# The relu of q written to the scores' PSUM banks in the last segments of a recurrent attention

## The chip, the cores and the metric

The kernel runs on one core of one Trainium2 chip. The core has five engines with a queue of instructions each: TensorE (PE in the profile, with its weight loads as PEld), VectorE (DVE), ScalarE (ACT), GpSimd (POOL) and SyncE (SP, which issues most transfers). Work passes between them through SBUF and, for the results of matmuls, through PSUM, which has eight banks of 512 fp32 columns in each of 128 partitions. The metric is device time in microseconds (us), smaller is better, as the median of several runs.

## What is computed

Two layers, each an attention and a mixture of experts, multiplied and added to x: `x = x + attention(norm(x)) * silu(experts(norm(x)))`. The change lies in the attention of the first layer. It has 16 heads of 64 columns; a sequence of 512 tokens is cut into 8 segments of 64, and a memory M with its sum Z is carried from one segment to the next. For each segment, in the reference:

```python
scores = jnp.einsum('bhid,bhjd->bhij', q, k) * scale      # masked above the diagonal
att_dot = jnp.einsum('bhij,bhjv->bhiv', jax.nn.softmax(scores, axis=-1), v)
sq = jax.nn.elu(q) + 1.0
att_mem = sq @ M / (sq @ jnp.swapaxes(Z, -2, -1))
sk = jax.nn.elu(k) + 1.0
M_new = M + jnp.einsum('bhld,bhlv->bhdv', sk, v)
Z_new = Z + sk.sum(axis=-2, keepdims=True)
att = gate * att_mem + (1.0 - gate) * att_dot
out = att.reshape(B, LSEG, H * DV) @ Wo
```

There are 4 sequences, so 32 segments, numbered 0 to 31 through all of them.

## The kernel before

The function `attn0` (line 599) goes through the 32 segments in one loop, `for n in range(nseg)` (line 854). Every instruction is issued through small helpers (`mm1`, `act1`, `vec1`), which keep the order in which the program is written for each engine; nothing is reordered. The profile therefore shows line 356 for all matmuls and line 359 for all ScalarE operations, and one goes by the names of tiles. The loop is a pipeline by hand: in iteration n the scores and the q side of segment n+1 are begun, the memory is read for n, the k side is prepared for n+1 and n+2, and the outputs of n-2 are transposed.

One iteration, in the order of the code, with the names that the profile uses:

- `elu_exp(n + 1, 0)` (line 699): ScalarE makes exp(q) in the tile `elu` and relu(q) in the tile `up`, 128 x 512 each, both in SBUF. Two buffers serve all `up` tiles, of q and of k in turn.
- `scores(n + 1)` (line 673): 16 small matmuls write `sc`; VectorE caps the result into the tile `E` (line 686).
- `memory(n)` (line 746): matmuls `mm` of elu(q) with the memory `mz`; VectorE takes the reciprocals (`rm`, line 743) and the quotients into `t` (line 744); GpSimd multiplies by the gate (line 763).
- `elu(n + 1, 0)` (line 706): VectorE forms min(exp(q), 1) + relu(q), reading `elu` and `up` (line 709). The sum is elu(q) + 1.
- `turned(n - 2, n + 1)` (line 712): transposes `tn`, evicted by ScalarE into `attT` (four small operations) and `sk`.
- `update(n)` (line 765): matmuls `mu`, and VectorE adds them to the memory `mz` (line 778).
- `attend(n)` (line 780): matmuls `dot` of the exponentiated scores with v; VectorE divides (`rd`, `t`) and keeps the sums (line 800); GpSimd multiplies and adds (lines 801 and 802).
- `elu_exp(n + 2, 1)`, then `scores_exp(n + 1)`, then `elu(n + 2, 1)`: ScalarE makes exp and relu of k for the segment after next and the exp of `E`; VectorE finishes elu(k).
- In every fourth iteration `output` (line 816) multiplies four segments by Wo: 32 matmuls `po`. In the last iterations that is n = 26 and n = 30.

So ScalarE's queue holds, in each iteration: exp and relu of q for n+1, four `attT`, `sk`, exp and relu of k for n+2, exp of `E`. Segments 7, 15, 23 and 31 are the last of their sequence and need no k side.

Matmul results go to PSUM tiles of two banks, [128, 2, 512], from the function `wide` (line 367). Four such tiles fill PSUM, and each new one takes the place that was given up longest ago:

```python
    def wide(self, name):
        bufs = 4 if self.four else 3
        return self.banks.tile([P, 2, S], F32, name=name, tag="w", bufs=bufs)
```

The scores need columns 0 to 255 of each of their two banks; columns 256 to 511 are not used. An instruction that writes to a tile waits until the tile's place is free, and an instruction that depends on another engine's waits for that engine's semaphore count.

Of the kernel before, what the change touches and what calls it, by code (L numbers as in the profile page):

```python
# [12 lines left out]
F32 = mybir.dt.float32  # L13
# [3 lines left out]
AF = mybir.ActivationFunctionType  # L17
ALU = mybir.AluOpType
# [3 lines left out]
P = 128  # L22
# [80 lines left out]
def bc(ap, axis, n):  # L103

    shape = list(ap.shape)
    return ap.unsqueeze(axis).to_broadcast(shape[:axis] + [n] + shape[axis:])


class Kernel:
# [257 lines left out]
# [4 lines that stand above are left out]
# [228 lines left out]
    def attn0(self, xnT, g0, stack, between):  # L599
# [4 lines left out]
        nc, tc = self.nc, self.tc  # L604
# [4 lines left out]
        pool = stack.enter_context(tc.tile_pool(name="a0", bufs=2))  # L609
# [9 lines left out]
        for k in range(4):  # L619
            t = pool.tile([P, 4, 2, DK + 1], F32, name=f"vone{k}", bufs=1)  # L620
# [3 lines left out]
        wide = self.wide  # L624
# [44 lines left out]
        def blocks(n, w):  # L669
            s = n % 4  # L670
            return qkv[n // 4][w][:, s * 8 : s * 8 + 8, :]

        def scores(n):

            q, k = blocks(n, 0), blocks(n, 1)
            ps = wide(f"sc{n}")
            for hp in range(4):
                for p in range(2):
                    for a in range(2):
                        self.mm1(  # L680
                            ps[halves[a], p, hp * 64 : hp * 64 + 64],
                            lhsT=k[halves[p], 2 * hp + a, :], rhs=q[halves[p], 2 * hp + a, :],
                            start=True, stop=True,
                        )
            e = pool.tile([P, 2, 4, LSEG], F32, name=f"E{n}", tag="E")
            self.vec1(nc.vector.tensor_tensor(  # L686
                e, ps[:, :, 0:256].rearrange("p x (hp c) -> p x hp c", hp=4),
                bc(bc(self.cap, 1, 4), 1, 2), ALU.min,
            ))
            seg[n]["e"] = e  # L690

        def scores_exp(n):
            e = seg[n]["e"]
            self.act1(e, e, AF.Exp, scale=1.0 / math.sqrt(DK))

        def last(n):
            return n % 8 == 7

        def elu_exp(n, w):
            t = pool.tile([P, 8, 64], F32, name=f"elu{w}{n}", tag=f"elu{w}")  # L700
            up = pool.tile([P, 8, 64], F32, name=f"up{w}{n}", tag="up")
            self.act1(t, blocks(n, w), AF.Exp)
            self.act1(up, blocks(n, w), AF.Relu)
            seg[n][w] = t, up

        def elu(n, w):

            t, up = seg[n][w]
            self.vec1(nc.vector.scalar_tensor_tensor(t, t, 1.0, up, ALU.min, ALU.add))  # L709
            seg[n][w] = t  # L710

        def turned(att=None, own=None):

            ps = wide(f"tn{att}_{own}").rearrange("p x (w hp c) -> p x w hp c", w=2, hp=4)
            each = [(0, hp, x) for hp in range(4) for x in range(2) if att is not None]
            each += [(1, hp, x) for hp in range(4) for x in range(2) if own is not None]
            for w, hp, x in each:
                if w:
                    src = seg[own][1][halves[x], 2 * hp : 2 * hp + 2, :].rearrange("d a j -> d (a j)")
                else:  # L720
                    src = seg[att]["att"][halves[x], hp].rearrange("i p v -> i (p v)")
                self.pin(nc.tensor.transpose(ps[:, x, w, hp], src, self.ident[halves[x], halves[x]]))  # L722
            if att is not None:
                attended(att, ps[:, :, 0])
            if own is not None:
                t = seg[own]["sk"] = pool.tile([P, 4, 2, DK], F32, name=f"sk{own}", tag="sk")
                self.act1(t, ps[:, :, 1].rearrange("p x hp d -> p hp x d"), AF.Copy)

        def values(n):

            for p in range(2):
                src = vd[n // 4][p].rearrange("(s hp r) d -> s r hp d", s=4, hp=4)
                nc.sync.dma_start(out=vone[n % 4][:, :, p, 0:DK], in_=src[n % 4])
# [12 lines left out]
        def memory(n):  # L746


            mz, sq = self.mz[(n % 8 + 1) % 2 + 1 if n % 8 else 0], seg[n][0]
            ps = wide(f"mm{n}")  # L750
            for hp in range(4):
                for p in range(2):
                    for a in range(2):
                        at = (2 * a + hp // 2) * (DK + 1)
                        self.mm1(
                            ps[halves[(a + hp) % 2], p, at : at + DK + 1],
                            lhsT=sq[halves[p], 2 * hp + a, :], rhs=mz[halves[p], hp, a, :],
                            start=True, stop=True,
                        )
            t = seg[n]["t1"] = pool.tile([P, 4, 2, DK], F32, name=f"t1{n}", tag="t1")  # L760
            r = pool.tile([P, 2, 4], F32, name=f"rm{n}", tag="rm")
            divided(ps, t.rearrange("p hp y d -> p y hp d"), r, heads(ps)[:, :, :, DK])
            nc.gpsimd.tensor_mul(t, t, self.gate)  # L763

        def update(n):

            old = self.mz[(n % 8 + 1) % 2 + 1 if n % 8 else 0]
            new = self.mz[n % 2 + 1]
            sk, v = seg[n]["sk"], vone[n % 4]
            ps = wide(f"mu{n}").rearrange("p a (hp c) -> p a hp c", hp=4)[:, :, :, 0 : DK + 1]  # L770
            for hp in range(4):
                for a in range(2):
                    for p in range(2):
                        self.mm1(
                            ps[halves[p], a, hp], lhsT=sk[halves[a], hp, p], rhs=v[halves[a], hp, p],
                            start=True, stop=True,
                        )
            self.vec1(nc.vector.tensor_tensor(new, old, ps.rearrange("d a hp v -> d hp a v"), ALU.add))
# [37 lines left out]
        def output(h):  # L816
            ps = wide(f"po{h}")
            for c in range(16):
                for p in range(2):
                    self.mm1(  # L820
                        ps[:, p, 0:D], lhsT=attT[h][halves[p], c].rearrange("v s x -> v (s x)"),
                        rhs=self.wo[halves[p], c, :],
                        start=(c == 0), stop=(c == 15),
                    )
            two = slice(h * 2, h * 2 + 2)
            gate = g0[h // 2][:, h % 2 * 2 : h % 2 * 2 + 2, :]
            sg = pool.tile([P, 2, D], F32, name=f"sg{h}", tag="sg")
            self.vec1(nc.vector.tensor_tensor(sg, ps[:, :, 0:D], gate, ALU.mult))
            nc.gpsimd.tensor_add(self.x[:, two, :], self.x[:, two, :], sg)
# [24 lines left out]
        for n in range(nseg):  # L854
            if n % 4 == 3:
                todo = project((n + 1) // 4 + 1)
            elif n == 0:
                todo = ahead
            each = 2 if n == 0 else 4 if n < 3 or n % 4 != 2 else 0
            nxt = n + 1 < nseg  # L860
            more = nxt and not last(n + 1)
            if n + 2 < nseg:
                values(n + 2)
            if nxt:
                elu_exp(n + 1, 0)
                scores(n + 1)
            memory(n)
            if nxt:
                elu(n + 1, 0)
            if n > 1 or more:  # L870
                turned(n - 2 if n > 1 else None, n + 1 if more else None)
            if not last(n):
                update(n)
            for f, *args in between.get(n - 0.5, []):
                f(*args)
            attend(n)
            ahead = n + 2 < nseg and not last(n + 2)
            if ahead:
                elu_exp(n + 2, 1)
            chunks, todo = todo[:each], todo[each:]  # L880
            for chunk in chunks[:1]:
                chunk()
            if nxt:
                scores_exp(n + 1)
            if ahead:
                elu(n + 2, 1)
            for chunk in chunks[1:]:
                chunk()
            for f, *args in between.get(n - 0.25, []):
                f(*args)  # L890
            if n % 4 == 2 and n > 4:
                output(n // 4 - 1)
            if not nxt:
                turned(n - 1)
            for f, *args in between.get(n, []):
                f(*args)
# [1677 lines left out]
```

## Time and profile before

| | us |
|---|---|
| median of 3 runs | 689.84 |
| lowest and highest run | 688.49 and 690.34 |
| time of the profiled execution | 691.6 |
| span in its trace | 689.9 |
| TensorE busy | 656.5 (95%) |
| VectorE busy | 501.9 (73%) |
| ScalarE busy | 487.2 (71%) |
| GpSimd busy | 349.1 (51%) |
| the 60 elu operations, line 709 | 47.5, 0.791 each |
| the 60 relu operations, `up` | 38.4, 0.640 each |

The first attention runs from about 80 to 313 us of the span; the experts of the second layer follow. Busy times are averages over stages with different limits, so the prediction reads the stretch around the last segments by itself. A line of a timeline gives the start in us, the duration in us, the engine, the line, the operation, the tiles (written <- read), the shape and the count; in square brackets stands the idle time just before it and what ended it. An fp32 matmul appears as two records, so 16 matmuls of `sc` are shown as x32, and the weight loads are left out. Matmuls are pipelined: the duration of a merged group reaches to the end of its last result, and the next group can start before. A releaser is inferred from semaphores: where it had long been done, another one is meant.

### The profile page before, as it was taken

To read this page: it belongs to the slowest core of one execution; us is meant where nothing else is said; L and a number is where in the kernel's file an instruction comes from. 1 tells how busy PE (TensorE), PEld (TensorE's weight loads), DVE (VectorE), ACT (ScalarE), POOL (GpSimd) and SP (SyncE) were. 2 spreads that over 40 slices of the span, in tenths; PEclk is the share of its full clock that TensorE was granted. 3 is DMA by queue.
4 is the path that set the end of the run, shared out by engine and by line. 5 is a ranking of instruction groups with operands and counts; after the bars stand their busy time and mean duration, and the time that the engine had idled before them with its cause. 6 is when DMAs were issued, how large, how long until landed. Compare 5 with 4: busy or idle time off the path is not lost.

```text
span 689.9 us, 23790 instructions
## 1 busy us (share of the span) xinstructions
PE 656.5 (95%) x10123; PEld 411.0 (60%) x10123; DVE 501.9 (73%) x1084; ACT 487.2 (71%) x806; POOL 349.1 (51%) x383
## 2 busy tenths in 40 slices
PE   8999999999999898899999999999999999999995
PEld 4666667988978768777778863333335243422424
DVE  6866476686677958865378225979898999678884
ACT  4433478797787787643554369988997999899850
POOL 7590046767767575873753243312584753321170
PEclk9999999999999999999999999999999999999998
DMA  6850153233233131100034359777849694956300
GB/s 169 155 149 0 68 150 96 49 110 95 51 105 99 35 95 34 34 2 1 4 122 159 96 164 251 204 192 162 236 153 212 154 243 133 223 137 164 77 17 20
DMA packets 85489, 79.72 MB, mean 116 GB/s; under 512 B 42640, under 2 KB 74160, under 8 KB 82304
## 3 DMA queue, kind: packets, MB, share of 16 engines
q1 hardware_dynamic: 82544, 75.39, 41.5%
q0 software_dynamic: 2256, 2.47, 1.9%
q8 instruction: 82, 1.34, 0.8%
q10 hardware_dynamic: 576, 0.26, 0.2%
q14 instruction: 31, 0.25, 0.1%
HBM read 51.62 MB, written 26.21 MB: 113 GB/s over the span
## 4 chain that ended last, share of the span: by engine, by line
PE 74%; DVE 14%; ACT 8%; DMA 2%; issue 1%; POOL 0%; SPq 0%; DVEq 0%; ACTq 0%; POOLq 0%
PE acc L356 9%; PE eo L356 8%; PE pp L356 7%; ACT e L359 7%; PE po L356 6%; PE ph L356 5%; PE pv L356 4%; PE b L356 3%; PE s L356 3%; PE pl L356 3%; PE dot L356 2%; PE pg L356 2%; PE pu L356 2%; PE sc L356 2%; DVE elu L709 2%; PE mu L356 2%
## 5 line engine op out<-in xcount | busy, mean ns | idle before, releaser
L359 ACT ACTIVATE e<-s 128x1024 f32<-128x1024 f32 x124 | 122.2, 1059 | 14.5 <-PE s L356 14.1
L356 PE MATMUL acc<-e,strip 128*32 128x512 f32 x1000 | 123.7, 598 | 0.9 <-DVE e L1969 0.9
L359 ACT ACTIVATE e<-e 128x1024 f32<-128x1024 f32 x104 | 107.4, 1095 | 0.0
L763 POOL TENSOR_TENSOR t<-t,gate 128x512 f32<-128x512 f32 x32 | 52.3, 1634 | 52.8 <-DVE t L744 52.8
L356 PEld LDWEIGHTS acc<-e,strip 128*32 128x32 f32 x1000 | 28.2, 109 | 70.0 <-issue 59.0
L801 POOL TENSOR_TENSOR t<-t,gate 128x512 f32<-128x512 f32 x32 | 50.1, 1566 | 25.9 <-DVE sums L800 22.2
L359 ACT ACTIVATE pj<-pp 128x512 f32<-128x512 f32 x64 | 38.5, 602 | 19.3 <-PE pp L356 17.7
L709 DVE SCALAR_TENSOR_TENSOR elu<-elu,up 128x512 f32<-128x512 f32 x60 | 47.5, 791 | 0.2
L359 ACT ACTIVATE h<-ph 128x1024 f32<-128x1024 f32 x20 | 20.5, 1025 | 35.9 <-PE ph L356 32.1
L356 PE MATMUL s<-q,k 64*128 64x512 bf16 x256 | 41.1, 382 | 3.6 <-ACT e L359 3.3
L356 PEld LDWEIGHTS <-k 64*128 64x128 bf16 x256 | 8.7, 94 | 59.9 <-issue 58.1
L802 POOL TENSOR_TENSOR t<-t,t 128x512 f32<-128x512 f32 x32 | 42.2, 1320 | 2.5
L686 DVE TENSOR_TENSOR E<-sc,cap 128x512 f32<-128x512 f32 x32 | 22.0, 688 | 29.0 <-PE sc L356 29.0
L356 PE MATMUL eo<-w_out,h 128*128 128x128 f32 x320 | 39.7, 278 | 0.0
L356 PEld LDWEIGHTS eo<-w_out,h 128*128 128x128 f32 x320 | 37.7, 192 | 3.4 <-issue 2.4
L359 ACT ACTIVATE elu<-pj 128x512 f32<-128x512 f32 x60 | 38.5, 642 | 0.1
L359 ACT ACTIVATE up<-pj 128x512 f32<-128x512 f32 x60 | 38.4, 640 | 0.0
L1750 POOL TENSOR_TENSOR pr<-pr,pr 128x512 f32<-128x512 f32 x14 | 22.5, 1632 | 30.5 <-DVE pr L1745 30.4
L359 ACT ACTIVATE attT<-tn 128x128 f32<-128x128 f32 x100 | 19.6, 282 | 20.9 <-PE tn L722 19.9
L356 PE MATMUL pp<-xnT,l0Wk 128*64 128x128 f32 x512 | 31.4, 280 | 3.0 <-issue 2.2
L1657 DVE TENSOR_TENSOR second<-second,first 128x1024 f32<-128x1024 f32 x16 | 26.7, 1672 | 9.6 <-DMA second<-qf 9.6
L356 PE MATMUL po<-l0wo,attT 64*128 64x128 f32 x512 | 31.9, 281 | 0.3 <-DVE t L744 0.3
(353 smaller groups left out, 1589.4 us busy)
## 6 DMA issues: line engine op xcount, KB each, us to landing
vd<-vt SPq DMA_DIRECT2D x32, 256.0 KB
vone<-vd SPq DMA_DIRECT2D x64, 128.0 KB
first<-qe SPq DMA_DIRECT2D x8, 1024.0 KB
second<-qf SPq DMA_DIRECT2D x16, 512.0 KB
third<-qf SPq DMA_DIRECT2D x32, 256.0 KB
qf<-qT SPq DMA_DIRECT2D x64, 64.0 KB
k<-kd SPq DMA_DIRECT2D x16, 256.0 KB
q<-qd SPq DMA_DIRECT2D x16, 256.0 KB
```

Of the source, the lines that this page charges most:

```text
L356: return self.pin(self.nc.tensor.matmul(*args, **kw))
L359: return self.pin(self.nc.scalar.activation(*args, **kw))
L686: self.vec1(nc.vector.tensor_tensor(e, ps[:, :, 0:256].rearrange("p x (hp c) -> p x hp c", hp=4), bc(bc(self.cap, 1, 4), 1, 2), ALU.min,))
L709: self.vec1(nc.vector.scalar_tensor_tensor(t, t, 1.0, up, ALU.min, ALU.add))
L763: nc.gpsimd.tensor_mul(t, t, self.gate)
L801: nc.gpsimd.tensor_mul(t, t, gate2)
L802: nc.gpsimd.tensor_add(t, t, seg[n]["t1"])
L1657: self.vec1(self.nc.vector.tensor_mul(t, t, self.first1[mm][:, two]))
L1750: self.nc.gpsimd.tensor_add(self.prod1[b, m], self.prod1[b, m], t)
```

## The change

For segments 27 to 31 (`n > 25` in the loop, where segment n + 1 is begun) the PSUM tile of the scores is taken before the exponentials, the relu of q is written to its unused columns 256 to 511 in both banks, and elu(q) reads it there. Exp of q stays in SBUF, and so does the k side. Segments 0 to 26 are as they were. The operations and their order on each engine stay the same; shapes are rewritten as views of two halves.

```diff
-        def scores(n):
+        def scores(n, ps=None):
             q, k = blocks(n, 0), blocks(n, 1)
-            ps = wide(f"sc{n}")
+            ps = ps or wide(f"sc{n}")
...
-        def elu_exp(n, w):
+        def elu_exp(n, w, bank=None):
             t = pool.tile([P, 8, 64], F32, name=f"elu{w}{n}", tag=f"elu{w}")
-            up = pool.tile([P, 8, 64], F32, name=f"up{w}{n}", tag="up")
             self.act1(t, blocks(n, w), AF.Exp)
-            self.act1(up, blocks(n, w), AF.Relu)
+            if bank is None:
+                up = pool.tile([P, 8, 64], F32, name=f"up{w}{n}", tag="up")
+                self.act1(up, blocks(n, w), AF.Relu)
+            else:
+
+                up = bank[:, :, 256:512].rearrange("p x (k d) -> p x k d", k=4)
+                self.act1(up, blocks(n, w).rearrange("p (x k) d -> p x k d", x=2), AF.Relu)
             seg[n][w] = t, up
 
         def elu(n, w):
             t, up = seg[n][w]
-            self.vec1(nc.vector.scalar_tensor_tensor(t, t, 1.0, up, ALU.min, ALU.add))
+            own = t.rearrange("p (x k) d -> p x k d", x=2) if len(up.shape) == 4 else t
+            self.vec1(nc.vector.scalar_tensor_tensor(own, own, 1.0, up, ALU.min, ALU.add))
             seg[n][w] = t
...
             if nxt:
-                elu_exp(n + 1, 0)
-                scores(n + 1)
+                bank = wide(f"sc{n + 1}") if n > 25 else None
+                elu_exp(n + 1, 0, bank)
+                scores(n + 1, bank)
             memory(n)
             if nxt:
                 elu(n + 1, 0)
```

## The prediction

> **What bounds the kernel now.** I read, in this order, the page's engine totals, its groups, the timelines of the four compute engines over the last segments of the first attention (272 to 308 us of the span), and the granted TensorE clock in short stretches there. The totals say that TensorE sets the whole, and the group table has the two operations that the change touches, 60 of each in all, of which it touches the last five:
>
> ```profile
> span 689.9 us, 23790 instructions
> PE 656.5 (95%) x10123; PEld 411.0 (60%) x10123; DVE 501.9 (73%) x1084; ACT 487.2 (71%) x806; POOL 349.1 (51%) x383
> ...
> L709 DVE SCALAR_TENSOR_TENSOR elu<-elu,up 128x512 f32<-128x512 f32 x60 | 47.5, 791 | 0.2
> ...
> L359 ACT ACTIVATE up<-pj 128x512 f32<-128x512 f32 x60 | 38.4, 640 | 0.0
> ```
>
> In the edited stretch it is different. The VectorE timeline (start, duration) runs without a gap from 281.3 to 299.7 us, and TensorE waits for it (`mm` of segment 29 below starts at 289.63, when the memory update of 288.81 has landed). Two elus of q there take 1.6 us where the others take 0.68; in both cases GpSimd is in the middle of an addition that reads SBUF (POOL lines), and VectorE moves on when it is over (287.07 + 1.26 = 288.33):
>
> ```profile
> 282.83 0.68 DVE L709 SCALAR_TENSOR_TENSOR elu<-elu,up 128x512 f32<-128x512 f32 x1
> ...
> 287.27 1.61 DVE L709 SCALAR_TENSOR_TENSOR elu<-elu,up 128x512 f32<-128x512 f32 x1
> ...
> 292.64 1.62 DVE L709 SCALAR_TENSOR_TENSOR elu<-elu,up 128x512 f32<-128x512 f32 x1
> ```
>
> ```profile
> 287.07 1.26 POOL L802 TENSOR_TENSOR t<-t,t 128x512 f32<-128x512 f32 x1
> ...
> 292.42 1.29 POOL L802 TENSOR_TENSOR t<-t,t 128x512 f32<-128x512 f32 x1
> ```
>
> ScalarE's timeline for iteration n=28 (it makes segment 29's q side): the transposes' evictions, sk, elu and relu of k, the scores' exp, and only then exp and relu of q. It is an unbroken row that starts when TensorE's transposes `tn` are there:
>
> ```profile
> 286.40 0.79 ACT L359 ACTIVATE attT<-tn 128x128 f32<-128x128 f32 x4
> 287.05 0.63 ACT L359 ACTIVATE sk<-tn 128x512 f32<-128x512 f32 x1
> ...
> 289.61 0.66 ACT L359 ACTIVATE up<-pj 128x512 f32<-128x512 f32 x1
> 291.76 0.79 ACT L359 ACTIVATE attT<-tn 128x128 f32<-128x128 f32 x4 [1.50 <-PE tn L722]
> ```
>
> And TensorE, where scores `sc` now run long before that relu: for segment 29 at 283.28 (its relu: 285.61 to 286.27), for 30 at 288.37 (relu 289.61 to 290.27), for 31 at 292.87 (relu 293.93 to 294.59):
>
> ```profile
> 276.78 3.84 PE L356 MATMUL po<-l0wo,attT 64*128 64x128 f32 x64 [0.30 <-DVE t L744]
> 280.56 0.69 PE L356 MATMUL sc<-pj,pj 64*64 64x64 f32 x32
> ...
> 283.28 0.75 PE L356 MATMUL sc<-pj,pj 64*64 64x64 f32 x32
> ...
> 288.37 0.65 PE L356 MATMUL sc<-pj,pj 64*64 64x64 f32 x32
> 289.63 0.70 PE L356 MATMUL mm<-mz,elu 64*64 64x65 f32 x32 [0.62 <-DVE rd L797]
> ...
> 292.87 0.69 PE L356 MATMUL sc<-pj,pj 64*64 64x64 f32 x32
> ...
> 297.76 5.00 PE L356 MATMUL po<-l0wo,attT 64*128 64x128 f32 x64
> ```
>
> **The change, part by part.** *Relu into PSUM* (ScalarE, five times). No row has ScalarE write to PSUM. Nearest are rows of the same size: SBUF to SBUF 0.66, PSUM to SBUF (`sk`) 0.63. I take no change; the bound is 0.1 us either way for each, 0.5 in all.
>
> *Elu from SBUF and PSUM* (VectorE, five times). The rows that read one operand from each, E (L686) and the memory update (L778), take 0.69 against 0.68, and none of them stretches beside a GpSimd operation. So each elu costs what it did, and the two stretched ones lose 1.61 - 0.68 = 0.93 and 1.62 - 0.68 = 0.94: a gain of 1.87 us if VectorE stays what sets the pace.
>
> *The wait.* In the changed program as built, the first `sc` matmul of segments 27 to 31 waits for ScalarE's count at that segment's relu of q; before, it waited for no ScalarE work of its own iteration. This is the wait to price. The columns are disjoint, and no row of before has two engines on one bank, so the trace alone would let one cost it at nothing: sum -1.87. The Trainium skill speaks against it (PSUM — Partial Sum Buffer, section "PSUM bank collisions raise a hardware error"): two engines at one bank and the same partitions collide even at other columns, and compilers order them. The waits of the built program are that order, so I price it as a serial wait. Behind `sc` in TensorE's order stand `mm`, `tn`, `mu`, `dot`; for `tn` waits ScalarE, whose last work is the next relu, for which the next `sc` waits. Two engines that worked side by side become one ring:
> - Segment 27 (n=26): relu ends at 273.48 + 0.62 = 274.10, so `sc` goes from 272.36 to 274.2. VectorE has other work until 275.03 and takes E at 275.05 as before: nothing lost. But the bank stays in use until the elu (276.55 + 0.68 = 277.23) and, in the built order, the output projection `po` takes it next; it waited for 276.64 and starts at 276.78, so +0.6. What follows it moves with it: `sc` of 28 to 281.15, whose relu ScalarE, idle for 4.3 us there, has ready.
> - From `sc` to the evictions: 282.40 - 280.56 = 1.84. From the evictions to the end of the relu: 285.61 + 0.66 - 282.40 = 3.87. With 0.1 for the hop, a ring of 5.8 us. Relu of 29 ends at 282.40 + 0.6 + 3.87 = 286.87, `sc` 286.95 (was 283.28); `sc` of 30 at 292.75 (was 288.37). In n=29 there is no k of a segment after 31, and the evictions reach the relu's end in 293.93 + 0.66 - 291.76 = 2.83: ring 4.77, `sc` of 31 at 297.5 (was 292.87).
> - E of 31 follows `sc` by 0.76 (281.32 - 280.56): 298.28, where VectorE had it at 295.90. The 1.87 us saved on the elus vanish in this wait. The built order gives `dot` of 30 the bank of `mm`, so it waits for L744's end, 1.59 after E (297.49 - 295.90): 299.87, start 300.0, and `po` half a microsecond later (a dot at full clock gives way to the next row after 0.5): 300.5. Before, without its slow clock, `po` would have come at 296.73 + 0.52 = 297.25. Loss: 3.2 us, all on TensorE.
>
> *The clock.* The granted clock of TensorE in neighbouring stretches of 3.4 us (busy, matmuls, clock, DMA share, GB/s):
>
> ```profile
> 286.60:290.00 3.40, 1.92 (x116) 1.00 0.03 5
> ...
> 293.40:296.80 3.40, 1.95 (x87) 1.00 0.00 0
> ...
> 296.80:300.20 3.40, 3.40 (x54) 0.50 0.02 5
> ```
>
> A stretch with 87 small matmuls is followed by one at half clock, one with 116 is not; the same happened at 259.3 after a stretch with 84. That is why `po` takes 5.00 instead of 3.84 and the `dot` before it 1.11 instead of 0.65: 1.6 us already paid. With the ring, TensorE works 3.0 us and stands still for 2.8 (284.15 to 286.95), 2.8 (289.95 to 292.75) and 1.75 (295.75 to 297.5). By these rows the border lies near 100 small matmuls in 3.4 us; a stretch that holds a gap of 2.8 us has room for (3.4 - 2.8) / 3.0 x 144 = 29 to, where the gap is cut in two, about 95. The Trainium skill's rule is looser (TensorE: Matmul & The Clock Gate, "Why this matters for your kernels": keep gaps under about 3 us; by it no gap here counts, and the sum stays +3.2). The row decides: gaps of 1.4 to 1.9 us did it. So after each long gap a half-clock stretch falls on `sc`, `mm`, `tn`, 1.8 us of the ring. Its place in the burst is chance: nothing to 1.7 us each, I take 1.0. Two more than before: +2.0. The third meets `dot` and `po` as before and cancels.
>
> **Sum.** +3.2 + 2.0 = +5.2 us. From there on TensorE is the bound (from 304 to 400 us it has no idle at all, and from there to its last matmul only some 8 us), in a fixed order, so the delay is kept. The profiled execution took 691.6 us for its span of 689.9; the runs' median is 689.84 with 688.49 to 690.34, so the sum made on the profile is carried over as a difference: 689.84 + 5.2 = 695.0.
>
> **The rivals.**
> - *Faster: VectorE goes on setting the pace* and the two stretched elus go: 689.84 - 1.87 = 688.0. For it: its unbroken row. Against: it decides only if each relu ends 0.76 us before VectorE can take E, that is by 285.0 for segment 29 and 290.4 for 30. It ends at 286.27 in the undisturbed trace for 29 already, and the ring moves it on. Chance 0.03.
> - *The wait without the clock*: gaps are counted otherwise than I read them, +3.2, 693.0 (692.2 to 693.8). Chance 0.20.
> - *The clock at its worst*: three stretches at half clock wholly on the path, 3.2 + 3 x 1.7 = 8.3: 698.1. Chance 0.08.
> - *The delay is caught up or the wait is void*: TensorE's 8 us of later idle are waits for ScalarE and VectorE, which move along; a transfer that paced the later stage would absorb it, but none shows among TensorE's waits. 689.8. Chance 0.07.
>
> **How the numbers follow.** The likeliest case, wait and clock, has 0.62 and gives 695.0, by itself 693.4 to 697.3. Within 0.3% (2.1 us), about what a measurement here can tell, falls the last rival, 0.07; faster the first, 0.03; slower the other three, 0.90. The range takes in the likeliest and the wait without the clock, and leaves out the worst clock and both rivals below: 692.2 to 697.5.
>
> **What would show it.** In the changed profile: elus of q in the last five at 0.68 with no stretched one; `sc` rows that start 0.1 after the relu's end, with TensorE idle for about 2.8 us before them, released by ScalarE; ScalarE's evictions 1.8 after each; gaps of 1 to 2 us ahead of E on VectorE; the `po` that starts at 297.76 now, at 300.5 or later; more than one half-clock stretch between 284 and 304. I am wrong if `sc` starts ahead of the relu, if the relu comes earlier in ScalarE's order than now, or if the clock stays at 1.00 through gaps of 2.8 us.

## The result, and the profile after

| | before | after |
|---|---|---|
| median | 689.4 (8 runs, 687.26 to 690.34) | 695.07 (8 runs, 692.88 to 697.65) |
| profiled execution, and its span | 691.6, 689.9 | 694.72, 693.0 |

All times are in us. The changed kernel is slower, with a ratio of 1.0087 (95% interval 1.0070 to 1.0105). A second set of runs gave 694.8 against 690.12, ratio 1.0072 (1.0059 to 1.0085). A new statement above moves later line numbers by 6 or 7: the elu is L715, the quotients L750, the GpSimd addition L808.

The group table of after, with the columns of before (busy time and mean ns, then the idle time ahead and its releaser), shows the two edited operations and the new wait of `sc`:

```profile
L715 DVE SCALAR_TENSOR_TENSOR elu<-elu,up 128x512 f32<-128x512 f32 x55 | 41.0, 746 | 0.2
L359 ACT ACTIVATE up<-pj 128x512 f32<-128x512 f32 x55 | 35.1, 639 | 0.0
L715 DVE SCALAR_TENSOR_TENSOR elu<-elu,sc 128x512 f32<-128x512 f32 x5 | 3.4, 677 | 0.0
L359 ACT ACTIVATE sc<-pj 128x512 f32<-128x512 f32 x5 | 3.1, 622 | 0.0
L356 PE MATMUL sc<-pj,pj 64*64 64x64 f32 x1024 | 23.1, 230 | 9.3 <-ACT sc L359 8.6
```

A relu into PSUM takes 622 ns on the mean, one into SBUF 639. The five elus of q take 677. TensorE now stands still for 8.6 us ahead of `sc`, waiting for ScalarE: four waits, the first of them (1.70) at segment 27. TensorE's timeline of after (start, duration; in brackets the idle time ahead) shows where:

```profile
277.50 3.84 PE L356 MATMUL po<-l0wo,attT 64*128 64x128 f32 x64
281.28 0.69 PE L356 MATMUL sc<-pj,pj 64*64 64x64 f32 x32
287.00 1.13 PE L356 MATMUL sc<-pj,pj 64*64 64x64 f32 x32 [2.45 <-ACT sc L359]
293.98 1.14 PE L356 MATMUL sc<-pj,pj 64*64 64x64 f32 x32 [2.69 <-ACT sc L359]
299.91 0.69 PE L356 MATMUL sc<-pj,pj 64*64 64x64 f32 x32 [1.72 <-ACT sc L359]
...
302.50 0.70 PE L356 MATMUL dot<-vone,E 64*64 64x65 f32 x32 [0.40 <-DVE t L750]
303.12 3.84 PE L356 MATMUL po<-l0wo,attT 64*128 64x128 f32 x64
306.89 0.70 PE L356 MATMUL mm<-mz,elu 64*64 64x65 f32 x32
```

ScalarE's timeline gives the other side. Each relu into the bank is over at the very start of an `sc` (286.32 + 0.63 = 286.95, `sc` at 287.00), and ScalarE then waits for the transposes that stand behind that `sc`:

```profile
283.12 0.79 ACT L359 ACTIVATE attT<-tn 128x128 f32<-128x128 f32 x4 [3.21 <-PE tn L728]
286.32 0.63 ACT L359 ACTIVATE sc<-pj 128x512 f32<-128x512 f32 x1
290.10 0.79 ACT L359 ACTIVATE attT<-tn 128x128 f32<-128x128 f32 x4 [3.15 <-PE tn L728]
293.30 0.63 ACT L359 ACTIVATE sc<-pj 128x512 f32<-128x512 f32 x1
297.07 0.78 ACT L359 ACTIVATE attT<-tn 128x128 f32<-128x128 f32 x4 [3.15 <-PE tn L728]
299.23 0.63 ACT L359 ACTIVATE sc<-pj 128x512 f32<-128x512 f32 x1
```

That is the ring: 5.72 us from `sc` of 28 to `sc` of 29, then 6.98 and 5.93, where 5.8, 5.8 and 4.77 had been worked out. The granted clock of after in neighbouring stretches of 3.41 us, laid so that they fit the half-clock stretches (length, busy and matmul records, clock, DMA share, GB/s), shows what makes the last two longer:

```profile
283.52:286.93 3.41, 0.89 (x46) 1.00 0.35 77
286.93:290.34 3.41, 3.34 (x92) 0.50 0.03 4
290.34:293.76 3.42, 0.95 (x64) 1.00 0.02 5
293.76:297.17 3.41, 3.19 (x88) 0.50 0.00 0
297.17:300.58 3.41, 1.69 (x108) 1.00 0.02 5
300.58:304.00 3.42, 3.02 (x122) 1.00 0.03 7
```

Each long gap fills most of a stretch, and the next stretch, which holds the burst, runs at half clock. After the third gap, with 108 records in its stretch, the clock stays.

Where the time went: `mm` of segment 31 starts at 306.89, and started at 302.69 before (+4.20). The delay stays at 4.2 until 446 us of the span of before, and is 2.90 from 472. This is hardly a recovery: variants below that are ahead, or less late, move by as much between the same two points (early_psum from -1.67 to -2.89, warm2_again from 1.03 to -0.29). Between them VectorE waits for a transfer for 2.90 us in before and 1.82 in after, so it is before's profiled execution that was long there.

### The profile page after: what moved, and what is told of

It reads as the page before. It is cut to its first block, busy times and chain, and to the rows that moved or that the text cites. A ratio compares the mean times of both kernels' runs of the same rounds, so it can differ in the third digit from the quotient of the medians.

```text
span 693.0 us, 23789 instructions
## 1 busy us (share of the span) xinstructions
PE 655.5 (95%) x10123; PEld 410.4 (59%) x10123; DVE 500.0 (72%) x1084; ACT 486.3 (70%) x806; POOL 346.4 (50%) x383
## 4 chain that ended last, share of the span: by engine, by line
PE 74%; ACT 11%; DVE 11%; issue 1%; DMA 1%; POOL 0%; SPq 0%; DVEq 0%; ACTq 0%; POOLq 0%
PE acc L356 10%; ACT e L359 8%; PE eo L356 8%; PE pp L356 7%; PE po L356 5%; PE ph L356 5%; PE pv L356 4%; PE b L356 3%; PE s L356 3%; PE pl L356 3%; PE sc L356 2%; PE dot L356 2%; PE den L356 2%; PE pg L356 2%; PE tn L728 2%; PE pu L356 2%
## 5 line engine op out<-in xcount | busy, mean ns | idle before, releaser
L808 POOL TENSOR_TENSOR t<-t,t 128x512 f32<-128x512 f32 x32 | 41.7, 1302 | 2.5
L715 DVE SCALAR_TENSOR_TENSOR elu<-elu,up 128x512 f32<-128x512 f32 x55 | 41.0, 746 | 0.2
L359 ACT ACTIVATE up<-pj 128x512 f32<-128x512 f32 x55 | 35.1, 639 | 0.0
L356 PE MATMUL sc<-pj,pj 64*64 64x64 f32 x1024 | 23.1, 230 | 9.3 <-ACT sc L359 8.6
```

Of the source, the lines that this page charges most:

```text
L356: return self.pin(self.nc.tensor.matmul(*args, **kw))
L359: return self.pin(self.nc.scalar.activation(*args, **kw))
L715: self.vec1(nc.vector.scalar_tensor_tensor(own, own, 1.0, up, ALU.min, ALU.add))
L808: nc.gpsimd.tensor_add(t, t, seg[n]["t1"])
```

## The experiments

The measure that I use beside the medians is the time from `sc` of segment 28 to `mm` of segment 31, read from TensorE's timeline. What was lost or gained earlier in an execution stays out of it (after_again is the changed kernel once more):

| kernel | `sc` of 28, 29, 30, 31 | `mm` of 31 | 28 to `mm` | half clock in it |
|---|---|---|---|---|
| before | 280.56, 283.28, 288.37, 292.87 | 302.69 | 22.13 | once, on `dot` and `po` (1.3 us) |
| after | 281.28, 287.00, 293.98, 299.91 | 306.89 | 25.61 | twice |
| after_again | 280.54, 286.27, 293.24, 299.17 | 306.14 | 25.60 | twice |
| wait_only | 281.45, 287.27, 294.34, 300.37 | 308.25 | 26.80 | four times |
| warm | 282.04, 289.73, 297.43, 302.12 | 309.10 | 27.06 | none |
| warm2 | 281.39, 287.12, 292.86, 297.55 | 304.53 | 23.14 | none |
| warm2_again | 280.61, 286.33, 292.06, 296.75 | 303.73 | 23.12 | none |
| one_29 | 281.21, 286.94, 291.11, 294.97 | 303.51 | 22.30 | once, after the wait |
| last_only | 280.79, 283.51, 288.60, 294.85 | 302.26 | 21.47 | none |
| early_psum | 280.99, 285.17, 289.35, 293.61 | 301.03 | 20.04 | none |
| early_psum_again | 279.52, 283.70, 287.88, 292.14 | 299.55 | 20.03 | none |
| early_sbuf | 281.22, 283.93, 289.05, 293.63 | 303.20 | 21.98 | once, on `mu`, `dot` and `po` |

Before's half clock costs 1.3 us here, and not the 1.6 that the prediction put down. `po` takes 1.16 us longer (5.00 against 3.84). That `dot` is slow ahead of it hardly counts, because `po` takes the place of `mm` and has to wait in any case until VectorE has read it. one_29, which has no half clock at this point, shows the wait (the quotients `t` end at 298.90 + 0.69 = 299.59):

```profile
299.74 3.84 PE L356 MATMUL po<-l0wo,attT 64*128 64x128 f32 x64 [0.21 <-DVE t L750]
```

In before the quotients end at 296.80 + 0.69 = 297.49. At full clock `po` would so have come at about 297.6, where the prediction had 297.25, and before would take about 20.8 us from `sc` of 28 to `mm` of 31 (an estimate: 22.13 less 0.13 and 1.16).

**The wait without the change of operands (wait_only).** The relu of q goes to SBUF and is read there as before; a tiny ScalarE operation writes two columns of each scores bank.

```diff
-                up = bank[:, :, 256:512].rearrange(...)
-                self.act1(up, blocks(n, w).rearrange(...), AF.Relu)
+                up = pool.tile([P, 8, 64], F32, name=f"up{w}{n}", tag="up")
+                self.act1(up, blocks(n, w), AF.Relu)
+                self.act1(bank[:, :, 256:258], blocks(n, w)[:, 0:2, 0:2], AF.Relu)
```

> The relu of q goes to SBUF and the elu reads it there, as before the change, but after it ScalarE writes two columns of each scores bank (a small extra relu whose result nobody reads), for segments 27 to 31. The scores' matmuls so wait for ScalarE as in the changed kernel. If the wait makes the loss: 694.5 to 696.5 us, like the changed kernel (695.1) plus at most 0.2 us for each of the small operations. If reading or writing the relu in PSUM makes the loss: 689 to 690, as before.

Measured: 695.38 against 689.64, ratio 1.0082 (1.0065 to 1.0099). Writing 4 elements a partition, 0.20 us long and outside the columns of the scores, costs what the whole change costs. ScalarE's and TensorE's timelines of this kernel:

```profile
287.02 0.20 ACT L359 ACTIVATE sc<-pj 128x4 f32<-128x4 f32 x1
294.08 0.20 ACT L359 ACTIVATE sc<-pj 128x4 f32<-128x4 f32 x1
```

```profile
287.27 1.13 PE L356 MATMUL sc<-pj,pj 64*64 64x64 f32 x32 [2.93 <-ACT sc L359]
294.34 1.13 PE L356 MATMUL sc<-pj,pj 64*64 64x64 f32 x32 [2.92 <-ACT sc L359]
300.37 1.13 PE L356 MATMUL sc<-pj,pj 64*64 64x64 f32 x32 [1.04 <-ACT sc L359]
```

The loss is the order of ScalarE ahead of `sc`. The run also takes away a false reading of after: its elus of q take 0.68 too, although they read `up` from SBUF. The ring has moved them out from under the GpSimd addition (in after, one elu starts at 290.00, and the addition is over at 287.84 + 1.28 = 289.12). So in after, 0.68 is no proof that PSUM freed them. The two runs do show the same hold-up from GpSimd's side. Its multiplication by the gate starts 0.16 us into such an elu in both; with the elu's operand in PSUM it takes 1.29 us (after, first row), with both operands in SBUF 1.65 (wait_only, second row):

```profile
290.16 1.29 POOL L769 TENSOR_TENSOR t<-t,gate 128x512 f32<-128x512 f32 x1 [1.05 <-DVE t L750]
290.43 1.65 POOL L770 TENSOR_TENSOR t<-t,gate 128x512 f32<-128x512 f32 x1 [1.14 <-DVE t L751]
```

**The ring with the clock kept up (warm, warm2, warm2_again, after_again).** After the attention dots in n=27 and n=28, matmuls of 512 fp32 columns write to the tile of that iteration's transposes, which ScalarE has read by then: five of them in warm, two in warm2. Nobody reads the result.

```diff
             attend(n)
+            if n in (27, 28):
+                for _ in range(5):       # 2 in warm2 and warm2_again
+                    self.mm1(seg[n + 1]["tn"][:, 0, :], lhsT=self.wqkv[0][:, 0:128],
+                             rhs=self.wqkv[0][:, 0:512], start=True, stop=True)
```

> The changed kernel with five extra fp32 matmuls of 512 columns (0.43 us each, results read by nobody) in TensorE's two long gaps ahead of the scores of segments 29 and 30. They fill 2.15 of some 2.6 us and delay nothing, since the scores wait for the relu anyway. If the half-clock stretches after the gaps cost what I forecast: the clock stays at 1.00 on both bursts, the ring is 5.8 instead of 7.0 us and the time falls by 2.0 to 2.4, to 692.8. If the clock is without effect on the path, or isn't held by this: 695 or more.

Measured: 696.71, ratio 1.0110 (1.0090 to 1.0130). The clock stayed at 1.00, but the expectation was missed by a mistake of mine: such a matmul shows as two records, and I had taken the time of one. Five took 4.56 us, and `sc` came 2.0 us after its relu, twice. With two the filler is over in time:

> The changed kernel with two more matmuls of 512 fp32 columns after the attention dots in n=27 and n=28, their result read by nobody. In the run with five of them the five took 4.56 us, so two take 1.8 us, inside the two gaps of 2.4 to 2.7 us: they must be over before the relu for which sc waits, and sc must start where it does in the changed kernel. Theory (ring of 5.8 us, and half-clock stretches that follow the gaps add 1.2 us a turn to it): granted clock 1.00 from 284 to 301, turns from sc to sc 5.8 and 4.8, about 692.7 us. Rival (the ring is as long as measured for another reason, a slower handover through the bank): turns stay at 7.0 and 5.9, about 695 us. Second rival: 1.8 us of work do not keep the clock; then half-clock bursts are seen as before, 695 to 696.5 us.

> The changed kernel itself, as the control beside the run with two filler matmuls per gap. As before: 5 to 6 us above the kernel before, turns of the ring of 7.0 and 5.9 where half-clock stretches fall on its bursts.

> The same kernel as in the run warm2 (two filler matmuls of 512 fp32 columns in each of the two gaps). There the ring ran as worked out (sc at 287.12, 292.86, 297.55, clock 1.00, mm of segment 31 2.4 us earlier than in the changed kernel), but the whole was no faster, and 5 us went at 385 us and later in gaps that no wait explains. If those gaps belong to that chip and not to the edit, this kernel is 2.3 us below the changed kernel, about 3 us above the kernel before. Rival: the filler itself costs later what it saves, then it equals the changed kernel or is above it.

TensorE's timeline of warm2_again:

```profile
280.61 0.69 PE L356 MATMUL sc<-pj,pj 64*64 64x64 f32 x32
283.81 1.98 PE L356 MATMUL tn<-l0Wq 128*128 128x512 f32 x4
286.33 0.69 PE L356 MATMUL sc<-pj,pj 64*64 64x64 f32 x32 [0.54 <-ACT sc L359]
289.54 1.98 PE L356 MATMUL tn<-l0Wq 128*128 128x512 f32 x4
292.06 0.69 PE L356 MATMUL sc<-pj,pj 64*64 64x64 f32 x32 [0.54 <-ACT sc L359]
296.75 0.69 PE L356 MATMUL sc<-pj,pj 64*64 64x64 f32 x32 [1.41 <-ACT sc L359]
```

The turns are 5.72, 5.73 and 4.69 us, and in warm2 5.73, 5.74 and 4.69: the ring as worked out (5.8, 5.8, 4.77), with full-speed bursts. From `sc` of 28 to `mm` of 31 it takes 23.1 against 25.6, so two half-clock stretches cost 2.5 us. The rival, a slower handover through the bank, falls. The medians bear it out in part. In the set with after_again, warm2_again has 693.61 (ratio 1.0061, 1.0044 to 1.0078) against 694.8 (1.0072, 1.0059 to 1.0085): 1.2 us less where 2.3 were expected, with intervals that overlap, and 3.0 us less in the spans of the profiled executions. The run warm2 itself gave 702.5 against 695.28 (1.0102, 1.0064 to 1.0140). The kernel before was slower there, on another chip, and TensorE lost time far behind the ring, in a row of small matmuls at 386 to 390 us that waits for nothing shown:

```profile
387.31 0.41 PE L356 MATMUL pl<-feat,strip 128*32 128x64 f32 x4 [0.52 <-issue]
388.72 0.30 PE L356 MATMUL pl<-feat,strip 128*32 128x129 f32 x2 [1.00 <-issue]
```

one_29 and last_only, of the same set, have such gaps in the same row; before, after and warm2_again have none there. What makes them was not tried. For this set I read the timelines more than the medians.

**One wait at a time (one_29, last_only).** The relu goes into the bank for segment 29 alone, or for 31 alone.

```diff
-                bank = wide(f"sc{n + 1}") if n > 25 else None
+                bank = wide(f"sc{n + 1}") if n == 28 else None    # n == 30 in last_only
```

> The relu of q goes into the bank for segment 29 alone. Ring theory: one wait alone is cheap, since the relu is not pushed on by a scores pass that waited before it. Its relu ends at 286.27 of the span, so sc of 29 starts at 286.35 instead of 283.28, E of 29 at 287.1 instead of 285.77 (+1.35), its elu takes 0.68 instead of 1.61 (-0.93): +0.4, about 690.0 us, with a half-clock stretch in the burst after the gap 691 us. Rival, every wait costs the same quarter of the loss of segments 28 to 31: 689.6 + 1.4 = 691.0 us with the clock at 1.00 and the gain of the elu already in it.

> The relu of q goes into the bank for segment 31 alone. Ring theory: the relu of 31 ends at 294.59, so sc of 31 starts at 294.7 instead of 292.87, and E of 31 could start at 295.45, before VectorE takes it at 295.90: nothing lost, elu of 31 takes 0.68 as before. About 689.6 us, 689.0 to 690.5 by the place of half-clock stretches. Rival, every wait costs a quarter of the loss: 691.0 us.

Measured: one_29 695.95 against 695.28, ratio 1.0013 (0.9998 to 1.0027); last_only 695.31, ratio 1.0013 (1.0000 to 1.0027). Scaled to 689.84 the ratio means 690.7 for both, with 689.7 to 691.7 and 689.8 to 691.7. For one_29 that holds both theories' numbers; for last_only it speaks more for the rival's 691.0 than for 689.6. The timelines say more. In one_29 `sc` of 29 came 5.73 us after that of 28 (5.79 expected), the burst after it fell on half clock, and `sc` of 30, which waits for no relu, followed in 4.17 us and not in 5.7: the ring doesn't close. The elu of q of 29 took 0.68. From `sc` of 28 to `mm` of 31 it takes 22.30, and before would take 20.8 without its half clock: 1.5 us for one wait and one half-clock stretch, where 0.4 and 1.0 had been put down.

In last_only `sc` of 31 came as expected (294.85 after 280.79 of 28: 14.06, where 294.7 - 280.56 = 14.14 had been worked out), and VectorE took `E` when it would have anyway. But "nothing lost" was wrong: 21.47 against 20.8 without half clock. The lost 0.6 us stands in TensorE's timeline of last_only:

```profile
294.85 0.69 PE L356 MATMUL sc<-pj,pj 64*64 64x64 f32 x32 [1.79 <-ACT sc L359]
295.37 0.65 PE L356 MATMUL mm<-mz,elu 64*64 64x65 f32 x32
296.34 0.70 PE L356 MATMUL mu<-vone,sk 64*64 64x65 f32 x32
297.87 0.70 PE L356 MATMUL dot<-vone,E 64*64 64x65 f32 x32 [0.83 <-DVE t L750]
```

The scores' tile is held until the elu, so the next tile takes another place. Here `dot` takes the place of `mm` and waits until VectorE has read it (297.03 + 0.69 = 297.72), though `dot` needs nothing of it.

**The same change in earlier segments (all_segs).** The condition is `n > 1`, so that segments 3 to 31 have it.

```diff
-                bank = wide(f"sc{n + 1}") if n > 25 else None
+                bank = wide(f"sc{n + 1}") if n > 1 else None
```

> The relu of q goes into the bank from segment 3 on, not from 27 on. Theory: in segments 3 to 26 TensorE has projection matmuls or other work in its queue and loses the wait only where none stands between; but in its fixed order they stand behind the waiting sc, so where the queue before sc is shorter than ScalarE's way to the relu, each wait costs. If the work before sc covers the waits there, about 695 us as in the changed kernel; if it does not, up to 24 waits of 1.4 us each, 728 us. I expect the cover to hold in most: 695 to 705 us.

Measured: 741.85 against 695.28, ratio 1.0688 (1.0664 to 1.0711). That the projection matmuls would cover most waits was wrong: TensorE takes its instructions in order, and the cover stands behind the waiting `sc`. The waits of TensorE in all_segs (total, times, longest):

```profile
PE sc L356 <- ACT sc L359: 42.1, 24, 2.4
```

The 24 waits of 1.75 us make 42.1 us, beside 46.6 lost. They are not parts of one sum: the kernel also runs nine stretches at half clock, 30.7 us together, where before has two, and some of the waits replace others that before has. What the clock alone costs here was not taken apart.

**The relu issued one iteration earlier (early_psum, early_sbuf).** If the order is the fault, the change should pay once the relu is done before `sc` comes. For segments 28 to 31 the relu of q is issued in the iteration before, after exp of k: into the bank in early_psum, into SBUF in early_sbuf. Segment 27 is as in the kernel before.

```diff
+        def relu_q(n, bank):             # to the bank, or to SBUF where bank is None
...
             if nxt:
-                bank = wide(f"sc{n + 1}") if n > 25 else None
-                elu_exp(n + 1, 0, bank)
-                scores(n + 1, bank)
+                if "up" not in seg[n + 1]:
+                    elu_exp(n + 1, 0)
+                scores(n + 1, seg[n + 1].get("bank"))
...
-            if ahead:
+            if n > 25 and n + 2 < nseg:
+                m = n + 2
+                seg[m]["bank"] = bank = wide(f"sc{m}")       # None in early_sbuf
...              exp k (if ahead), relu_q(m, bank), relu k (if ahead), exp q
+            elif ahead:
                 elu_exp(n + 2, 1)
```

> Relu of q in PSUM for segments 28 to 31 (27 as before the change), but ScalarE makes it earlier in its order: after sk and the exp of k, ahead of the relu of k, the exp of q and the exp of E, in the iteration before. If the place of the relu in ScalarE's order makes the loss: the ring is cut to 1.84 + 2.3 + 0.1 = 4.2 us, below VectorE's own 4.4, TensorE waits no longer, the two stretched elus of 1.6 us are gone: 687.5 (689.4 less 1.87). If any wait of the scores for a relu in their bank costs, wherever it stands: 691 to 695.

> The control of the run with the early relu: the same new order on ScalarE for segments 28 to 31, but the relu goes to SBUF. If the order alone is neutral and only the PSUM operand frees the elu from GpSimd: 689.4 as before, with elus of 1.6 us. If the order alone brings the gain: 687.5 to 688.5.

> The relu of q in the bank for segments 28 to 31 with the relu issued one iteration earlier, once more beside the others: 1.5 to 2 us below the kernel before (ratio 0.9975).

Measured: early_psum 687.98 against 689.64, ratio 0.9975 (0.9966 to 0.9984), and again 688.27 against 690.12, ratio 0.9974 (0.9965 to 0.9984); early_sbuf 690.02, ratio 1.0007 (0.9992 to 1.0022). The order alone gains nothing; with it, the change gains 1.7 to 1.9 us and beats both kernels. Here is the proof for VectorE that after lacked. VectorE's and GpSimd's timelines of early_psum have both elus of q inside a GpSimd addition, and not stretched:

```profile
287.81 0.68 DVE L724 SCALAR_TENSOR_TENSOR elu<-elu,sc 128x512 f32<-128x512 f32 x1
292.24 0.68 DVE L724 SCALAR_TENSOR_TENSOR elu<-elu,sc 128x512 f32<-128x512 f32 x1
```

```profile
287.60 1.28 POOL L817 TENSOR_TENSOR t<-t,t 128x512 f32<-128x512 f32 x1
292.02 1.27 POOL L817 TENSOR_TENSOR t<-t,t 128x512 f32<-128x512 f32 x1
```

and those of early_sbuf have them stretched, under the same additions:

```profile
288.04 1.60 DVE L724 SCALAR_TENSOR_TENSOR elu<-elu,up 128x512 f32<-128x512 f32 x1
293.40 1.62 DVE L724 SCALAR_TENSOR_TENSOR elu<-elu,up 128x512 f32<-128x512 f32 x1
```

```profile
287.82 1.27 POOL L817 TENSOR_TENSOR t<-t,t 128x512 f32<-128x512 f32 x1
293.19 1.28 POOL L817 TENSOR_TENSOR t<-t,t 128x512 f32<-128x512 f32 x1
```

The Trainium skill (SBUF — State Buffer, section "SBUF: two separate sides") tells of a port pair that VectorE and GpSimd share as a lock: a VectorE operation with two SBUF inputs waits for a GpSimd operation that reads SBUF. The rows agree: 1.60 with both operands in SBUF, 0.68 with one in PSUM. Of the 1.94 us between 21.98 and 20.04, about 1.0 is early_sbuf's half clock: 0.70 on `po` (4.54 against 3.84) and, by the same estimate as for before, 0.3 ahead of it, for `po` came at 298.73 and could have come at 298.4, after the quotients (297.56 + 0.69 = 298.25). Some 0.9 is left of the 1.86 on the elus; early_psum has three short waits of `sc` in the same stretch (0.97, 0.54, 0.24). Against before without its half clock early_psum is 0.8 ahead (20.04 against 20.8). The medians differ by more, 1.7 to 1.9; what makes the rest was not taken apart.

**Early in every segment (early_all).** As early_psum, from segment 6 on.

```diff
-            if n > 25 and n + 2 < nseg:
+            if n > 3 and n + 2 < nseg:
```

> As early_psum, but from segment 6 on, and not from 28 on. With the late relu in every segment each of 24 waits cost 1.75 us (42.1 us in the waits of TensorE). Theory: the loss lies in the order, relu behind the evictions that wait for TensorE, so issued one iteration earlier the relu is there when sc comes, and the 42 us of waits go: within 2 us of the kernel before, either way, since TensorE is the bound in these segments and a faster elu buys nothing there. Rival: the bank, now in use from the iteration before to the elu, makes other tiles wait for a place, 0.6 us or more for each of 22 segments, 13 us above the kernel before or more.

Measured: 704.66 against 690.12, ratio 1.0198 (1.0166 to 1.0230). The waits of `sc` for ScalarE are gone, but others take their place. Lines of TensorE's waits in early_all:

```profile
PE dot L356 <- DVE t L759: 4.0, 6, 1.4
PE pv L356 <- DVE rd L812: 3.3, 3, 1.9
PE pv L356 <- ACT vt L359: 1.8, 2, 1.2
PE mu L356 <- ACT vt L359: 1.8, 1, 1.8
PE sc L356 <- ACT sc L359: 1.7, 3, 1.0
```

In before, `dot` waits 0.3 for the quotients in all, and `pv` and `mu` show no such releasers. In early_all TensorE also runs at half clock in five stretches of 3.4 us, 17 us together, where before has two. The rival is near in size (13 us were named); how much of it is places in PSUM, how much ScalarE's new order and how much the clock was not taken apart.

## Why the prediction was right

The time came as put down, 695.07 for 695.0, by the mechanism put down: one wait closes a ring between two engines, and the ring's gaps cost clock. That it came so close is in part luck: the ring was put 0.3 us too dear and the clock 0.5 too cheap, the medians of the two sets lie 0.5 above and 0.5 below the sum of 5.2, and between the profiled executions the loss up to `mm` of 31 is 4.1.

- *Relu into PSUM*: no change was taken; 0.622 on the mean against 0.639, inside the bound of 0.1.
- *Elu from SBUF and PSUM*: the five take 0.677, as put down. But wait_only has 0.68 with SBUF operands too, so in after the ring and not the PSUM operand decides. That the operand frees the elu is shown by early_psum beside early_sbuf only. Even there some 0.9 of the 1.87 us arrive on TensorE's path.
- *The wait*: right, and shown by wait_only. `sc` was forecast at 274.2, 281.15, 286.95, 292.75, 297.5; warm2, where the clock stays up, has 274.34, 281.39, 287.12, 292.86, 297.55, and `po` at 300.76 for 300.5. The forecast 3.2 us have two parts. The place taken over from the scores of 27 was put at 0.6: between the projection at 268.7 us and `po` at 277 after falls back by another 0.6 (0.11 to 0.72), last_only and one_29, with no edit there, by none. The ring's part was put at 2.6 and is 23.1 - 20.8 = 2.3. The difference is the 297.25 of the prediction: it read at n = 26 that `po` waits for the quotients, and left the same wait out at n = 30.
- *The skill's rule on PSUM collisions* (PSUM — Partial Sum Buffer, "PSUM bank collisions raise a hardware error") weighed against the trace that showed no wait: the order decided. The tiny write to other columns has the same wait. Whether the chip would bear the collision was not tried.
- *The clock*: two more half-clock stretches were right for the two long gaps (286.93 and 293.76), and they cost 2.5, not 2.0: 1.2 each where I took 1.0 between nothing and 1.7. The skill's looser rule (TensorE: Matmul & The Clock Gate, section "Why this matters for your kernels": no idle gaps over about 3 us) would have given 693.0. Gaps of 2.45 and 2.69 us were enough, and without half clock the same ring (warm2_again) stays 2.5 us shorter.
- The steps that failed: "The third meets `dot` and `po` as before and cancels", and "1.6 us already paid". The third gap had 108 records in its stretch, and no half clock followed; what before had paid was 1.3. Between the profiled executions the edit therefore costs 0.6 + 2.3 + 2.5 - 1.3 = 4.1 up to `mm` of 31, as measured (4.20 - 0.11). The medians differ by 5.67 and 4.68. A kernel before that pays no half clock there gives 0.6 + 2.3 + 2.5 = 5.4, and the granted clock of the executions without a trace speaks for it. Each has its mean on record, and one stretch of 3.41 us at half clock takes 0.0025 off it (3.41 x 0.5 / 690). Of 59 executions of before (32 beside wait_only, 27 beside after_again), 25 have 0.998 or 0.999, which leaves hardly room for one such stretch; the profiled one has two of them, besides a piece at its very end as every trace here has, and a mean of 0.992, with only four of the 59 as low. The 13 executions of the changed kernel have 0.985 to 0.995. On the mean this is 0.996 against 0.991, or 3.7 us of clock lost: about two stretches. So "two more than before" holds on the mean, not because a third cancels, but because before mostly pays less than its profile shows. At which microsecond those stretches lay is not shown.
- *Sum*: that the delay is kept was right up to 446 us. Of the rivals, "faster" needed the relu earlier than ScalarE's order has it; early_psum gives it that and ends at 688.0, the rival's own number. That is partly chance, since only 0.8 to 0.9 of the rival's 1.87 us is seen on TensorE's path.

## What to carry to other kernels

An unused part of a PSUM bank is not free space: whoever writes it becomes a predecessor of everything that uses the bank, and holds its place longer, however few columns are written. Before putting work there, look up where the writer stands in its own engine's order; if what stands ahead of it waits for the engine that will now wait, two engines that ran side by side become a ring, and cover that stands behind the wait in the queue covers nothing. Here writing the relu to the bank lost 5 us or gained 1.7 with its place in ScalarE's order, and cost 14 us and more when spread to segments where TensorE was the bound.

## What the runs showed of the hardware

- The granted clock does not follow busy time alone. The half-clock stretches of one execution lie on a fixed grid of 3.41 us. Of the stretches at full clock on that grid, those with 40 (one_29), 46 and 64 (after), 59 (after_again), 88 (before; 1.96 us busy) and 90 records (early_sbuf; 1.92 us) of small matmuls were followed by half clock; those with 95 (last_only; 2.16 us), 98 (after_again; 1.62 us), 108 (after; 1.69 us) and 115 (one_29; 1.92 us) were not. Some records can be missing from a trace, so the border is not sharp. For large matmuls the count is not the measure: a stretch of warm2_again with 48 records and 2.76 us busy, fillers among them, kept the clock. The way back looks alike, at other numbers: half-clock stretches with 80 and 78 such records (wait_only) were followed by half clock again, those with 84 (wait_only, after_again), 88 and 92 (after) by full clock.
- A matmul of 512 fp32 columns takes 0.9 us at full clock and shows as two records (4.56 us for five).
- VectorE and GpSimd hold each other up when both read SBUF: a 128 x 512 elu with both operands in SBUF takes 1.60 us beside a GpSimd addition, with one in PSUM 0.68 (early_sbuf, early_psum); a GpSimd multiplication beside such an elu takes 1.65 and 1.29 (wait_only, after).
- ScalarE writes a 128 x 512 result to PSUM in 0.62 us, to SBUF in 0.64.
